# Constants fetched by SyncE in the order of need, the first and last graph's score rows made by TensorE, and the last attention split, in a planned two-layer graph-attention kernel

## The chip, the cores and the metric

The kernel runs as one program on one core of a Trainium2 chip. The core has a tensor engine (PE), a vector engine (DVE), a scalar engine (ACT), a GpSimd engine (POOL) and a sync engine (SP), each with its own stream of instructions, and 16 DMA engines that all queues share. SP, ACT and POOL can issue DMAs. The metric is the device time of one execution in microseconds. Before the change three runs gave 3724.74, 3729.95 and 3728.39 us, with the median 3728.39.

## The reference

There are B = 32 graphs with N = 512 nodes and D = 512 features each, all in float32, and for every graph an integer adjacency of 512 x 512. Two layers follow each other, each in a residual form.

```python
h = relu(layernorm(x))                                    # layer 0
s = (h @ w_src)[:, :, None] + (h @ w_dst)[:, None, :] + attn_b
att = softmax(where(adj + eye == 0, -inf, leaky_relu(s, 0.2)), axis=-1)
x = x + einsum('bij,bjh->bih', att, h)

h = relu(layernorm(x))                                    # layer 1
def gat(x, W, a_src, a_dst, bias):                        # H heads of F features
    xl = (x @ W).reshape(B, N, H, F)
    e = leaky_relu((xl . a_src)[:, :, None, :] + (xl . a_dst)[:, None, :, :], 0.2)
    att = softmax(where((adj > 0) | eye, e, -1e9), axis=1)
    return einsum('bsdh,bshf->bdhf', att, xl) + bias
h = elu(gat(h, W1, ...))                                  # W1 512 x 1024, 4 heads of 256
x = x + gat(h, W2, ...)                                   # W2 1024 x 512, 1 head of 512
```

So each graph has six attentions over 512 x 512 pairs of nodes (one in layer 0, four heads and one more in layer 1), and two products with weights.

## The kernel before

**Per graph.** Nodes lie in T = 4 row blocks of 128 partitions. `layer0_scores` (L695) takes the layernorm statistics of x (L479), writes the normalised and rectified rows h (ACT, L496), makes two score columns for each row block by dot products on DVE (`dot`, L363), loads the adjacency and calls `edge_weights`. `layer0_out` (L714) aggregates and adds to x. `layer1_in` (L719) normalises x again, transposes it on PE into hT, adds b2 to x on POOL and stores x into a DRAM buffer ("spill"). `layer1_project` (L838) multiplies by W1, `layer1_scores` and `layer1_head` (L857, L869) do the attention of a head, its elu and the transposition of its result. `layer2_project` (L912) multiplies by W2, `load_back` (L748) fetches x from DRAM again, and `layer2_out` (L932) does the last attention on it and stores the graph's rows to the output.

**The products with weights** (`products`, L756; the matmul is L808) use seven half-size products in place of eight: four sums of quarters of the left side, made by DVE or POOL (L789, L790), and seven weight factors 11, 21, 22, T1, T2, T3, -T4, of which four are sums made once at the start (`sums`, L449). The products run in that list's order, from 11 to -T4, and results are copied or added out of PSUM (L506, L821). The weights carry two more columns per head, a weight times its attention vector, so that the scores of a node come out of the same product; `scores_1` (32 dots over W1) and `scores_2` (32 over W2, and 8 small sums) make these columns on DVE at the start.

**An attention** (`edge_weights`, L570) needs, for every pair of nodes, the sum of a column value (per partition) and a row value. The two score columns (`ac`) are turned into rows through DRAM: `in_lines` (L535) transposes the columns on PE, copies them to SBUF (`e`) and stores them as lines in DRAM; `row_of` (L552) fetches a line broadcast to all 128 partitions, 256 KB. The row `a_row` is copied by ACT into a PSUM bank (`in_bank`, L564, the copy is L567). DVE adds the mask to it and takes the maximum of each row (L579, four times), then two small steps (L584, L586) give the bound m per node. PE spreads m over the partitions by four transposes of a broadcast column (`spread`, L518; the transpose is L473) into `m_bank`. ACT makes leaky_relu of row plus column from `c_row` (L596), DVE subtracts m (L599), POOL adds the mask, a large negative number where there is no edge (L601), and ACT takes the exponential (L604). `aggregate` (L607, matmul L614) multiplies the weights E by the values; a column of ones beside the values yields the divisor. In `attend` (L621) DVE takes its reciprocal (L626) and adds the quotient to x (L632). Layer 1 does the same for a head with L876 and L879, then ACT's exponential (L888) and DVE's minimum and maximum (L891).

**Masks.** POOL's queue loads an adjacency, converted to bf16 on the way (L650). `masks0` adds the identity to the diagonal blocks (L667) and makes the mask by one DVE operation (L670); `masks1` does it by L682 and L688. SP transposes masks by DMA (`transposed_mask`, L652), four transfers for each.

**What sets the order.** No engine's instructions are written in their final order. Every operation is recorded by `op` with the engines that can do it, a modelled cost (the time its engine is occupied, and the time until its result is there), what it reads and writes, a rank (its position, less `ahead`), and a mark `lock` for operations of DVE and POOL that the model lets exclude each other. `Plan.run` makes six drafts: each is a list scheduling by the modelled costs, in which buffers of a kind are given out as they come free (for most kinds in a fixed turn), and the rank for the next draft is the latest time at which an operation would have to start by the draft before (`latest`). The draft with the shortest modelled end is emitted in its order. Thus a changed cost anywhere can change the order of all engines from beginning to end. In the model each engine is a resource; DMA queues of SP and ACT are two more (SP, ACTQ), and a DMA's bytes occupy nothing: it has only an issue time and a landing time.

**The sequence of recording** is at the end of the kernel (L953 to L988): x of graph 0, the constants, graph 0's layer 0, the weight sums, then a loop over graphs in which the projection of graph b, the last attention of graph b - 1, the four heads of b, layer 0 of b + 1 and b + 2 and the second projection of b are interleaved. A 33rd pass of the loop does only the last attention of graph 31. SBUF has two x buffers, one `h`, one `xl2` and three `pair`; PSUM has six `acc` banks, one `a_bank` and one `m_bank`.

**Constants.** `load_constants` (L371) issues the layer 0 vectors, the attention vectors and the biases from ACT's queue (nine transfers) and the weights from SP (W1 in 8 transfers, W2 in 16).

## Time and profile before

| | |
|---|---|
| runs | 3724.74, 3729.95, 3728.39 us; median 3728.39 |
| the profiled execution | 3721.97 us, of which the span of the profile is 3720.2 us |
| PE (matmul) busy | 3626.9 us, 97% of the span |
| PEld (weight loads) busy | 3134.7 us, 84% |
| DVE busy | 2846.8 us, 77% |
| ACT busy | 1803.5 us, 48% |
| POOL busy | 1627.4 us, 44% |
| DMA | 313.22 MB, mean 84 GB/s |

The span runs from the first to the last profiled event, and the execution's own time is a little longer. PEld overlaps PE. A line such as "15.25 0.29 DVE L667 ... [3.23 <-DMA m<-in_adj_dram]" is an instruction of the timeline: start, duration, engine, source line, operation, output and inputs, and in brackets how long its engine stood idle before it and what ended that. SPq and ACTq rows are the issue of a DMA. A line of waits reads: engine, output and source line that waited, what released it, then the sum in us, the number of such waits and the longest. A line of windows gives a stretch in us and the busy time and count of PE, PEld, DVE, ACT and POOL in it, then the granted clock of the tensor engine as a share of its full speed, the busy share of the DMA engines and the GB/s that they moved.

### The profile page before, as it was taken

The numbers are of one execution on the slowest core, as the hardware profiler recorded it, in microseconds if no ns is written. First come the engines' busy times: TensorE is split into PE (matmuls) and PEld (weight loads), VectorE is DVE, ScalarE is ACT, GpSimd is POOL, SyncE is SP. The second block draws the span as 40 slices with busy tenths as digits, with TensorE's granted clock in tenths as the row PEclk, the third lists the DMA queues.
The fourth block names the chain that finished last, engine by engine and source line by source line (L and its number), as shares of the span: only waits on it lengthen the run. The fifth ranks groups of instructions, "written<-read, shape, count | busy, mean of one in ns | idle before, by whom it ended". The sixth has DMA issues, their size and how long they took to land.

```text
span 3720.2 us, 51279 instructions
## 1 busy us (share of the span) xinstructions
PE 3626.9 (97%) x17792; PEld 3134.7 (84%) x17792; DVE 2846.8 (77%) x7339; ACT 1803.5 (48%) x3339; POOL 1627.4 (44%) x1383
## 2 busy tenths in 40 slices
PE   3899999999999999999999999999999999999998
PEld 2788888888888888888888888888888888888887
DVE  6987778877778777778877787777887777788755
ACT  2454454554445554445544545544455544455433
POOL 3444444444445434444444444444454444444432
PEclk9999999999999999999999999999999999999999
DMA  5244323343323343233443233432233432334311
GB/s 143 65 102 103 72 72 90 75 103 93 71 80 83 85 102 74 77 84 76 101 103 71 73 90 75 103 92 70 80 82 87 103 74 78 83 74 103 91 49 37
DMA packets 305045, 313.22 MB, mean 84 GB/s; under 512 B 150672, under 2 KB 189072, under 8 KB 304784
## 3 DMA queue, kind: packets, MB, share of 16 engines
q1 hardware_dynamic: 269696, 273.49, 27.0%
q0 software_dynamic: 33792, 33.56, 6.9%
q8 instruction: 140, 2.29, 0.3%
q10 hardware_dynamic: 1296, 2.88, 0.2%
q14 instruction: 121, 0.99, 0.1%
HBM read 241.96 MB, written 67.90 MB: 83 GB/s over the span
## 4 chain that ended last, share of the span: by engine, by line
PE 88%; DVE 4%; DMA 3%; ACT 2%; POOL 2%; issue 1%; DVEq 0%; ACTq 0%; POOLq 0%; SPq 0%
PE acc L614 42%; PE acc L808 38%; PE acc L473 5%; PE m_bank L473 2%; DMA m<-in_adj_dram 2%; POOL E_one L601 1%; ACT E L596 1%; DVE junk L364 1%; DMA c_row<-lines 1%; DVE junk L579 1%; DVE E L599 1%; ACT E L604 1%; POOL E L601 0%; PE acc L541 0%; DVE E_one L599 0%
## 5 line engine op out<-in xcount | busy, mean ns | idle before, releaser
L601 POOL TENSOR_TENSOR E<-E,m 128x512 f32<-128x512 f32 x512 | 608.4, 1213 | 856.2 <-DVE E L599 851.6
L614 PE MATMUL acc<-pair,E 128*128 128x257 f32 x4096 | 960.2, 380 | 1.0 <-ACT E L604 0.9
L614 PEld LDWEIGHTS acc<-pair,E 128*128 128x128 f32 x4096 | 751.1, 189 | 104.1 <-ACT E L604 7.7
L808 PE MATMUL acc<-w_T,E 128*128 128x257 f32 (+1 forms) x2048 | 525.7, 380 | 0.0
L614 PE MATMUL acc<-h,E_one 128*128 128x256 f32 (+1 forms) x2048 | 478.9, 381 | 5.2 <-ACT E_one L604 5.2
L614 PE MATMUL acc<-xl,E_one 128*128 128x257 f32 (+1 forms) x2048 | 464.5, 380 | 2.7 <-ACT E_one L604 2.7
L579 DVE CUSTOM_DVE_ANT_0 junk<-m1T,a_bank 128x512 bf16<-128x512 bf16 x640 | 436.5, 682 | 35.1 <-ACT a_bank L567 20.0
L604 ACT ACTIVATE E<-E 128x512 f32<-128x512 f32 x512 | 318.7, 622 | 252.0 <-POOL E L601 250.2
L614 PEld LDWEIGHTS acc<-h,E_one 128*128 128x128 f32 x2048 | 385.7, 191 | 59.7 <-ACT E_one L604 5.9
L614 PEld LDWEIGHTS acc<-xl,E_one 128*128 128x128 f32 x2048 | 384.3, 190 | 59.9 <-ACT E_one L604 3.1
L808 PEld LDWEIGHTS acc<-w_T,E 128*128 128x128 f32 x2048 | 377.0, 190 | 53.2
L596 ACT ACTIVATE E<-c_row,ac 128x512 f32<-128x512 f32 x512 | 343.9, 707 | 3.6 <-DMA c_row<-lines 3.6
L599 DVE TENSOR_TENSOR E<-E,m_bank 128x512 f32<-128x512 f32 x512 | 327.4, 678 | 2.8 <-PE m_bank L473 1.8
L506 ACT COPY xl<-acc 128x257 f32<-128x257 f32 x226 | 84.6, 374 | 502.1 <-PE acc L808 501.8
L506 ACT COPY pair<-acc 128x258 f32<-128x258 f32 x421 | 155.8, 370 | 342.6 <-PE acc L808 342.2
L888 ACT ACTIVATE e<-v,minus_one 128x512 f32<-128x512 f32 x256 | 183.5, 717 | 232.2 <-DVE v L879 172.0
L650 POOL DMA_DIRECT2D m<-in_adj_dram x64 | 51.7, 808 | 546.9 <-DVE col L579 501.4
L632 DVE SCALAR_TENSOR_TENSOR x<-acc,r,x 128x256 f32<-128x256 f32 x512 | 239.5, 479 | 62.1 <-PE acc L614 54.3
L891 DVE SCALAR_TENSOR_TENSOR v<-e,v 128x512 f32<-128x512 f32 x256 | 267.9, 1047 | 13.2 <-ACT e L888 11.4
L808 PE MATMUL acc<-w,hT 128*128 128x258 f32 x1024 | 273.5, 382 | 0.7 <-DVE pair L821 0.6
L808 PE MATMUL acc<-w,pair 128*128 128x257 f32 x1024 | 258.1, 379 | 0.0
L808 PE MATMUL acc<-w,E 128*128 128x257 f32 (+1 forms) x1024 | 254.6, 380 | 0.0
(98 smaller groups left out, 5885.3 us busy)
## 6 DMA issues: line engine op xcount, KB each, us to landing
a_row<-lines SPq DMA_DIRECT2D x192, 256.0 KB, 3.3
c_row<-lines SPq DMA_DIRECT2D x192, 256.0 KB, 3.4
x<-in_x_dram SPq DMA_DIRECT2D x32, 1024.0 KB, 8.5
m<-in_adj_dram POOLq DMA_DIRECT2D x64, 512.0 KB, 7.6
spill<-x SPq DMA_DIRECT2D x32, 1024.0 KB, 4.3
x<-spill SPq DMA_DIRECT2D x32, 1024.0 KB
out_dram<-x SPq DMA_DIRECT2D x32, 1024.0 KB, 5.1
m0T<-m SPq DMA_TRANSPOSE x128, 7.4
```

Source lines behind the costliest of these rows:

```text
L473: op("PE", on_pe(P, transpose=True), lambda: nc.tensor.transpose(dst_of(), src_of(), identity), src, dst(part), ahead)
L506: nc.scalar.copy(dst_of(), src_of())
L579: lambda t=t: nc.vector.tensor_tensor_reduce(junk, mask_max.at[:, t, :], a_row.at, 1.0, LOWEST, ALU.add, ALU.max, accum_out=amax.at[:, t : ...
L596: lambda t=t: nc.scalar.activation(E.at[:, t, :], c_row.at, AF.Prelu, bias=a_of(t), scale=1.0, alpha=SLOPE),
L599: op("DVE", on_dve(N), lambda t=t: nc.vector.tensor_sub(E.at[:, t, :], E.at[:, t, :], m_row.at), m_row(*ROW) + E(t), E(t))
L601: "POOL", on_pool(N, True), lambda t=t: nc.gpsimd.tensor_add(E.at[:, t, :], E.at[:, t, :], mask.at[:, t, :]),
L604: op("ACT", on_act(N), lambda t=t: nc.scalar.activation(E.at[:, t, :], E.at[:, t, :], AF.Exp), E(t), E(t))
L614: lambda s=s: nc.tensor.matmul(acc.at[:, :n], E.at[:, s, node_block(t)], of(s), start=(s == 0), stop=(s == T - 1)),
L632: lambda acc=acc, r=r, f=f, t=t: nc.vector.scalar_tensor_tensor(X.at[:, t, f], acc.at[:, :HD], r.at, X.at[:, t, f], op0=ALU.mult, op1=ALU. ...
L808: lambda k=k: nc.tensor.matmul(acc.at[:, :width], at[a]()[:, k, node_block(r)], weight_of(w, k, c), start=(first and k == 0), stop=(k == n ...
L888: op("ACT", on_act(2 * F, 1), lambda e=e, ts=ts: nc.scalar.activation(e.at, v.at[:, ts, :], AF.Exp, bias=minus_one), parts, e(0))
L891: lambda e=e, ts=ts: nc.vector.scalar_tensor_tensor(v.at[:, ts, :], e.at, 1.0, v.at[:, ts, :], op0=ALU.min, op1=ALU.max),
```

## The change

The planner gets another model of transfers. A DMA that moves data now carries a third cost, its bytes at 300 bytes per ns (`by_dma`), and these occupy one shared resource one after the other (`moving`); of the last `IN_FLIGHT` = 8 transfers the oldest must have landed before another is issued. ACT's own DMA queue is gone from the model.

All constants are fetched by SP. The three small ones of layer 0 are recorded ahead (`AHEAD` = 400), W1 and its attention vectors in their place, and b1, b2, the attention vectors of layer 2 and W2 behind (`LATER` = 300). W2 comes in four transfers in place of 16.

For layer 0 of graph 0 and the last attention of graph 31 the way through DRAM is left out: with `lines` None, `edge_weights` makes both rows by `spread`, four PE transposes each, a into `a_bank` and c into an `acc` bank, and ACT's L596 reads c from PSUM.

The last attention of graph 30 is recorded in two halves: its first two row blocks (`EARLY`) in the loop as before, the other two behind the second projection of graph 31. Then follow the fetch of graph 31's x and its last attention. Graph 31's second projection writes into a `pair` buffer in place of `xl2` (its column of ones is set by a POOL memset), so that graph 30's values can stay. For these last two graphs each row block has an output transfer of its own, 256 KB, in place of one of 1024 KB for a graph.

The operations of the other graphs are the same; their order comes out of the new plan. Lines behind the change have other numbers in the changed kernel: L473 becomes L487, L496 L510, L579 L591, L586 L598, L596 L609, L599 L612, L601 L614, L604 L617, L614 L627, L808 L822, L891 L905.

```diff
-            occupied, there = self.cost(draft, i)
+            occupied, there, *moves = self.cost(draft, i)
             if locks and e in lock:
                 at = max(at, lock["POOL" if e == "DVE" else "DVE"])
                 lock[e] = at + occupied
+            for held in moves:
+                if len(landed) >= self.IN_FLIGHT:
+                    at = max(at, landed[-self.IN_FLIGHT])
+                moving = max(moving, at) + held
+                there += moving - at
+                landed.append(at + there)
...
+def by_dma(n, after=2000.0):
+    return 350.0, after, n / 300.0
...
+    AHEAD, LATER = 400, 300
     QUARTER = (("11", "T1"), ("21", "22"))
     def load_constants():
-        def fetch(queue, ns, place, src, token):
-            engine = {"SP": nc.sync, "ACTQ": nc.scalar}[queue]
-            op(queue, (70.0, ns), lambda: engine.dma_start(place(), src), (), token)
-        fetch("ACTQ", 4000.0, lambda: ws_r, rows(w_src, D), W["w0"](0))
-        fetch("ACTQ", 4000.0, lambda: wd_r, rows(w_dst, D), W["w0"](1))
-        fetch("ACTQ", 4000.0, lambda: b0_r, rows(attn_b, 1), W["w0"](2))
+        def fetch(n, place, src, token, ahead):
+            op("SP", by_dma(4 * P * n), lambda: nc.sync.dma_start(place(), src), (), token, ahead)
+        fetch(D, lambda: ws_r, rows(w_src, D), W["w0"](0), AHEAD)
+        fetch(D, lambda: wd_r, rows(w_dst, D), W["w0"](1), AHEAD)
+        fetch(1, lambda: b0_r, rows(attn_b, 1), W["w0"](2), AHEAD)
         att = [Buffer("E"), Buffer("E")]
         for i, vector in enumerate((att_src1, att_dst1)):
-            fetch("ACTQ", 12000.0, lambda i=i: flat(att[0])[:, i * HF : (i + 1) * HF], rows(vector, HF), att[0](i))
+            fetch(HF, lambda i=i: flat(att[0])[:, i * HF : (i + 1) * HF], rows(vector, HF), att[0](i), 0)
         w1_k = w1.rearrange("(k p) (h f) -> k p h f", p=P, f=F)
         w2_k = w2.rearrange("(k p) f -> k p f", p=P)
         for k in range(KD):
             for half, q in enumerate(QUARTER[k // (KD // 2)]):
                 fetch(
-                    "SP", 10000.0 + 2000.0 * k, lambda k=k, q=q: w1_s[q][:, k % (KD // 2), :, 2:],
-                    w1_k[k, :, half::2, :], W["w1"]((q, k % (KD // 2))),
+                    H // 2 * F, lambda k=k, q=q: w1_s[q][:, k % (KD // 2), :, 2:], w1_k[k, :, half::2, :],
+                    W["w1"]((q, k % (KD // 2))), 0,
                 )
-        fetch("ACTQ", 20000.0, lambda: b1_r, rows(b1, HF), W["b1"](1))
-        fetch("ACTQ", 20000.0, lambda: b2_r, rows(b2, D), W["b2"](0))
+        fetch(HF, lambda: b1_r, rows(b1, HF), W["b1"](1), -LATER)
+        fetch(D, lambda: b2_r, rows(b2, D), W["b2"](0), -LATER)
         for i, vector in enumerate((att_src2, att_dst2)):
-            fetch("ACTQ", 20000.0, lambda i=i: flat(att[1])[:, i * D : (i + 1) * D], rows(vector, D), att[1](i))
-        for k in range(KH):
-            for half, q in enumerate(QUARTER[k // (KH // 2)]):
+            fetch(D, lambda i=i: flat(att[1])[:, i * D : (i + 1) * D], rows(vector, D), att[1](i), -LATER)
+        nk = KH // 2
+        w2_q = w2.rearrange("(i k p) f -> i p k f", p=P, k=nk)
+        for i in range(2):
+            for half, q in enumerate(QUARTER[i]):
                 fetch(
-                    "SP", 16000.0 + 1000.0 * k,
-                    lambda k=k, q=q, half=half: w2_s[q][:, k % (KH // 2), :] if half else w2_s[q][:, k % (KH // 2), 2:],
-                    w2_k[k, :, W2 - 2 :] if half else w2_k[k, :, : W2 - 2], W["w2"]((q, k % (KH // 2))),
+                    nk * HD, lambda q=q, half=half: w2_s[q] if half else w2_s[q][:, :, 2:],
+                    w2_q[i, :, :, W2 - 2 :] if half else w2_q[i, :, :, : W2 - 2], W["w2"](*((q, k) for k in range(nk))), -LATER,
                 )
         op(
...
-        a_row = in_bank("a_bank", row_of("a_row", lines, k))
+        a_row = spread("a_bank", scores, a_of, AHEAD) if lines is None else in_bank("a_bank", row_of("a_row", lines, k))
...
         m_row = spread("m_bank", m(0) + E("place"), lambda t: m.at[:, t : t + 1], AHEAD)
-        c_row = row_of("c_row", lines, k + 1)
+        c_of = lambda t: ac.at[:, k + 1, t : t + 1]
+        c_row = spread("acc", scores + E("place"), c_of, AHEAD) if lines is None else row_of("c_row", lines, k + 1)
...
-                E(s) + values(part(s)) + result("place"), acc(0),
+                E(s) + values(*part(s)) + result("place"), acc(0),
             )
...
-                "SP", (2300.0, 6000.0),
+                "SP", (2200.0, 3000.0, 600.0),
...
-        L0[b] = (h0, edge_weights("E_one", scores, ac, in_lines(ac, scores, 2), 0, m0, m0T))
+        L0[b] = (h0, edge_weights("E_one", scores, ac, in_lines(ac, scores, 2) if b else None, 0, m0, m0T))
...
-        xl = Buffer("xl2")
+        xl = Buffer("xl2" if b < B - 1 else "pair")
+        if b == B - 1:
+            op("POOL", (110.0, 120.0), lambda: nc.gpsimd.memset(xl2_of(xl)[:, :, 2 + D :], 1.0), (), xl(2))
...
-        L2[b] = (edge_weights("E_one", ac(0), ac, in_lines(ac, ac(0), 2), 0, m1T, m1), xl)
-    def layer2_out(b):
-        E, xl = L2.pop(b)
-        Xb = X.pop(b)
-        attend(E, Both(xl), lambda s: s, 2, Xb)
-        op(
-            "SP", (100.0, 5000.0), lambda: nc.sync.dma_start(node_tiles(out, b), Xb.at),
-            Xb(*((t, half) for t in range(T) for half in range(2))), (),
-        )
-    class Both:
-        def __init__(self, buf):
-            self.buf = buf
-        at = property(lambda self: self.buf.at)
-        def __call__(self, s):
-            return self.buf((0, s), (1, s))
+        L2[b] = (edge_weights("E_one", ac(0), ac, in_lines(ac, ac(0), 2) if b < B - 1 else None, 0, m1T, m1), xl)
+    def xl2_of(buf):
+        return buf.at if buf.kind == "xl2" else buf.at[:, : T * (2 + D + 1)].rearrange("p (t f) -> p t f", t=T)
+    def layer2_out(b, ts=ROW, whole=True):
+        E, xl = L2[b]
+        Xb = X[b]
+        attend(E, xl, lambda: xl2_of(xl), lambda s: ((0, s), (1, s), 2), 2, Xb, ts)
+        for block in (ROW,) if whole else [[t] for t in ts]:
+            op(
+                "SP", by_dma(4 * P * len(block) * D),
+                lambda block=block: nc.sync.dma_start(
+                    node_tiles(out, b)[:, block[0] : block[-1] + 1, :], Xb.at[:, block[0] : block[-1] + 1, :]
+                ),
+                Xb(*((t, half) for t in block for half in range(2))), (),
+            )
+    EARLY = T // 2
...
-    for b in range(B + 1):
-        if b < B:
-            masks1(b)
-            layer1_project(b)
+    for b in range(B):
+        masks1(b)
+        layer1_project(b)
         if b:
             load_back(b - 1)
-            layer2_out(b - 1)
-        if b == B:
-            break
+            layer2_out(b - 1, ROW if b < B - 1 else ROW[:EARLY], b < B - 1)
...
+    layer2_out(B - 2, ROW[EARLY:], False)
+    load_back(B - 1)
+    layer2_out(B - 1, ROW, False)
```

## Prediction

> **What bounds the kernel now.** I read the page first, for the bound. Then the waits of PE in three stretches, the windows, and the timelines of start and end.
>
> ```profile
> span 3720.2 us, 51279 instructions
> PE 3626.9 (97%) x17792; PEld 3134.7 (84%) x17792; DVE 2846.8 (77%) x7339; ACT 1803.5 (48%) x3339; POOL 1627.4 (44%) x1383
> ```
>
> The tensor engine is the bound: 97% busy, and the change takes no matrix product away. Only the 3% in which PE has nothing to do can be won. Where do they lie? PE's waits between 190 and 3600 us (first three lines) and before 190 us (the rest):
>
> ```profile
> PE acc L614 <- ACT E L604: 0.9, 5, 0.2
> PE m_bank L473 <- DVE col L586: 0.8, 1, 0.8
> PE acc L541 <- DVE ac L707: 0.2, 1, 0.2
> PE acc L541 <- DVE ac L707: 37.8, 1, 37.8
> PE m_bank L473 <- DVE col L586: 19.8, 2, 18.5
> PE acc L808 <- DVE pair L821: 6.3, 2, 5.6
> PE acc L473 <- ACT h L496: 5.6, 1, 5.6
> PE acc L614 <- ACT E_one L604: 5.2, 2, 2.7
> ```
>
> In 3410 us of middle, PE waits 1.9 us. The idle time is the start and the end. Windows of start and end (busy us of each engine with its count, granted clock, DMA share, GB/s):
>
> ```profile
> 0.00:60.60 60.60, 1.50 (x6) 0.82 (x6) 32.69 (x106) 8.24 (x12) 13.30 (x20) 1.00 0.74 202
> 60.60:186.00 125.40, 109.83 (x495) 92.72 (x496) 111.08 (x312) 56.28 (x103) 62.84 (x48) 0.92 0.24 56
> 3683.40:3697.70 14.30, 5.09 (x24) 3.76 (x22) 6.44 (x16) 4.98 (x10) 1.87 (x2) 0.80 0.11 37
> 3697.70:3720.20 22.50, 16.35 (x64) 13.62 (x64) 4.45 (x12) 1.89 (x3) 2.62 (x3) 0.88 0.13 47
> ```
>
> From 60.6 to 186 us DVE is busy 111.08 of 125.4 us, 89%: there it is nearly as full as PE. The timeline of the start, each line a step of the chain:
>
> ```profile
> 15.25 0.29 DVE L667 TENSOR_TENSOR m<-m,ident 128x128 bf16<-128x128 bf16 x1 [3.23 <-DMA m<-in_adj_dram]
> 21.04 1.28 ACT L496 ACT_TABLE_LOAD   x1 [21.04 <-DMA w<-in_L_gnn_W_dram]
> 30.27 0.69 DVE L479 BATCH_NORM_STATS2 st<-x 128x6 f32<-128x512 f32 x1 [12.95 <-DMA x<-in_x_dram]
> 40.05 0.46 SPq L547 DMA_DIRECT2D lines<-e  x1
> 52.77 0.69 DVE L579 CUSTOM_DVE_ANT_0 junk<-m,a_bank 128x512 bf16<-128x512 bf16 x1 [0.15 <-DVE junk L364]
> 60.58 15.62 PE L614 MATMUL acc<-h,E_one 128*128 128x257 f32 x64 [2.75 <-ACT E_one L604]
> ```
>
> ACT issues loads until 21 us, so its table load and the first normalised rows come late. DVE then stands 12.95 us before the second graph's x. The row's transfer waits until 40.05 us on SP behind three DMA transposes (36.03, 3.92 long). The maximum stands behind weight products on DVE until 52.77. The end:
>
> ```profile
> 3690.50 0.69 DVE L579 CUSTOM_DVE_ANT_0 junk<-m1T,a_bank 128x512 bf16<-128x512 bf16 x1 [2.66 <-ACT a_bank L567]
> 3693.84 1.11 PE L473 MATMUL m_bank<-ident,col 128*128 128x128 f32 x4 [6.46 <-DVE col L586]
> 3697.70 16.35 PE L614 MATMUL acc<-xl,E_one 128*128 128x257 f32 x64 [2.75 <-ACT E_one L604]
> 3714.60 0.39 SPq L938 DMA_DIRECT2D out_dram<-x  x1
> ```
>
> PE is idle 6.46 and 2.75 us, then runs partly at half clock, and 5.6 us follow the last DMA issue.
>
> **Start: the new chain to the first attention.** ACT loses its nine issues; table load and L496 (2.92 us for four) fit before the masks. DVE's order becomes: statistics of graph 0; the first adjacency's diagonal; then the mask of the second adjacency, which is a new wait, with everything of graph 0 queued behind it; the mask of the first; eight score products; two statistics of x of graph 1; the four L579; two more statistics; the maximum. So the unknown is T, the landing of the second adjacency. The first lands at 15.25. Issue to landing is 13.7, 19.8 and 23.9 us for the three first ones; the second is issued at about 2.4 us, so lands near 22.2. T lies between 15.3 and 22.2: fewer bytes go ahead of it now (no attention vectors of layer 2, no b1 and b2, which move behind the weights), but x of graph 1 comes forward to fifth. I take 19.
>
> T 19.0; two masks 2 x 0.69 = 1.4; score products 31.48 to 37.44 = 6.0; bias and handover to PE 0.4; four TensorE transposes at cold clock 1.1 (the 1.11 of m_bank), handover 0.1; four L579, 52.77 to 55.65, 2.9; two statistics 2 x 0.62 = 1.2; two small ones 0.4 (3693.42 to 3693.84); from m_bank to the first product 56.72 to 60.58 = 3.9, and 0.2 for two weight products before the subtraction. Sum 36.6, against 60.58: 24 us earlier (21 to 28 with T). The second four transposes, for c, end 0.9 us later; ACT's four L596 (2.56) end near 31.7, before the subtraction needs them. L596 now reads PSUM: ACT's copies of 128x512 take 0.58 from SBUF (L567) and 0.59 from PSUM (hT), so 0.0 more. The DMA transposes of m0 stand on SP before the last weight piece and wait for the mask at 20.4; four issues of 1.25 and 2.5 to landing make about 28 to 31, needed at 34.7. Behind that wait on SP stand one piece of W1, b1, W2, b2 and the layer 2 vectors, wanted only after 55 us; POOL's next load is not behind it.
>
> **What of the 24 us stays.** DVE had done 32.7 us of work by 60.6. By 36.6 it has done about 20 (the steps above). The 12.7 us left, chiefly 30 of 32 W1 products at 0.47, move under the first attention and into the stretch where DVE was 89% busy. To the state of 186 us DVE's work is 32.7 + 111.1 = 143.8, so 123.8 remain at 36.6. At 89% that takes 139 and 10 us are won; at 100%, 123.8 and 25.6, more than the 24. DVE has 75 of 93 us from 186 on, so some of it can run over into the middle; I take 94%, nearer to the 92.6% (86.10 of 93) of its fullest slice: 132, state reached at 168.3, gain 18 (10 to 24). The two fewer ACT copies and six fewer small DMAs of graph 0 and 31 lie off the path.
>
> **Middle.** Thirty graphs have the same instructions in another order. W2 in four transfers for sixteen frees 12 issues of 0.43 on SP, once. The split last attentions cost no more products. I cost the middle at 0; the cover is that PE's waits there sum to 1.9 us while DVE has 18 us per 93 free.
>
> **End.** Gone: e copy, the line's transfer (1.2), the row's (3.07), a_bank's copy (0.60). Before, from the last -T4 product's end (3683.4) to 3697.7 is 14.3. After: two copies 0.8, ac copy 0.2, handover 0.3, transposes 0.6 warm, L579s 2.9, one added eviction sum 0.43, two small 0.4, then 3.9: 9.6 us, 4.7 less. Against it: after the last -T4, 16 products remained before; now 8, as its place in PE's order is later: 8 x 0.217 = 1.7. Net 3.0 (1 to 4.7). The second half of graph 30's last attention, held back, would be cover for this hole, but in the instruction order it stands before the last heads' attention, and nothing of it in the hole: 0.
>
> Clock: the 64 last products take 16.35 for 64 x 0.217 = 13.9, so 2.4 are lost to half clock, and 0.5 in m_bank. PE's idle pieces become about 3.1 and 3.4 us. Gain 0 to 2.9; 1.2 taken, as 2.75 us of idle shows no switch of its own and 5.6 to 6.5 does.
> The Trainium skill, page "TensorE: Matmul & The Clock Gate", section "Part 1: The HAM clock gate", says a free-running window of about 3.4 us must be idle before the clock is halved. The 6.46 us hole with clock 0.80 agrees; by the rule two pieces of 3.1 and 3.4 would seldom halve it, and the gain would be 2.9.
>
> Output: the last transfer is 256 KB in place of 1024 KB. From issue to end 5.6; a 256 KB row takes 3.07 and 0.5 remains: 2.0 less (0 if only latency counts, 2.5).
> Against splitting speaks the skill, page "DMA: Bandwidth & Descriptors", section "Bandwidth": make transfers of 1 MiB or more. Three of the four go out beside products, so only the last one's length would matter, and by its fit (2.0 us plus bytes over 436 GB/s, an estimate) that is 1.8 less.
>
> **Sum.** 18 + 3.0 + 1.2 + 2.0 = 24.2 us. The profiled execution took 3721.97 (span 3720.2); that gives a span of 3696. It lies 6.4 below the median of the three runs, 3728.39, so in their terms 3704. A measurement tells 0.2% (7.5 us) from no change.
>
> **Rivals.**
> A, slower: the new order brings a wait in every graph. Place: PE's transposes of the maximum (m_bank) behind DVE in the heads, where the order sets a head's L579s between the divisions, activations and minima of the head before. An SBUF operation of DVE stretches beside POOL: L891 is 0.69 alone, 1.05 on average, and one POOL mask addition is 1.21. One such wait unlucky per graph, 1.0 us x 30 = 30: 3704 + 30 = 3734. It turns the sign from 0.8 us per graph. For: the wait already peeps out (0.8 us once), and the old order has been free of it. Against: 18 us of free DVE per 93.
> B, little: DVE stays at 89% through the start, or T is beyond 22: 10 us there and 3 at the end, 3715.
> C: the start gains all 24 and the clock stays up: 24 + 3 + 2.9 + 2 = 32, 3696.
>
> **Chances.** Forecast with C, 3694 to 3714: 0.60. B, 3714 to 3724: 0.20. A, 3721 to 3745: 0.20. Likeliest 3704. The range 3693 to 3731 leaves out half of A, half of a tenth below: under 0.2. Faster: 0.60 + three fifths of B = 0.72, less 0.02 for an unforeseen wait: 0.70; same 0.11; slower 0.19.
>
> **What would show it.** First L614 product (L627 after) at 33 to 40 us; DVE's one wait at the start for an adjacency near 19; no ACT wait for a weight; DVE over 90% busy from 37 to 165; at the end no row transfer, about 10 us from last -T4 to attention, four output transfers of 256 KB. Wrong if PE's waits in the middle exceed 20 us in sum, or the first attention comes after 45.

## The result and the profile after

The changed kernel takes 3693.76 us (median; 3693.08 to 3694.85) against 3726.71 us before (four runs, 3724.74 to 3729.95): a ratio of 0.9911, with the 95% interval 0.9894 to 0.9928. That is 33 us, or 0.9%, faster; the prediction said 3704.0 us, with a range of 3693 to 3731. The profiled execution took 3694.24 us and its span is 3692.5 us, 27.7 us less than the 3720.2 of before. The two differences are not the same number, and that is taken up below.

The page after:

```profile
span 3692.5 us, 51317 instructions
PE 3625.2 (98%) x17806; PEld 3131.3 (85%) x17806; DVE 2878.2 (78%) x7478; ACT 1760.2 (48%) x3227; POOL 1592.1 (43%) x1353
```

PE's busy time is the same within 1.7 us; what went is time in which it had nothing to do. Its waits before 190 us:

```profile
PE a_bank L487 <- DVE junk L378: 26.7, 4, 25.2
PE m_bank L487 <- DVE col L598: 12.9, 4, 5.1
PE acc L487 <- ACT h L510: 7.0, 1, 7.0
PE acc L627 <- ACT E_one L617: 5.3, 2, 2.7
```

The wait for the first score columns begins at zero and ends at 25.2 us, where PE makes the first row itself. Before, PE's first work was at 37.8 us, followed by 18.5 us of waiting for the maximum; now the wait for the maximum is 4.1. The start in lines of the timeline:

```profile
14.08 0.29 DVE L680 TENSOR_TENSOR m<-m,ident 128x128 bf16<-128x128 bf16 x1 [5.24 <-DMA m<-in_adj_dram]
20.80 0.69 DVE L695 TENSOR_SCALAR m<-m 128x2048 bf16<-128x2048 bf16 x1 [4.84 <-DMA m<-in_adj_dram]
22.12 6.62 SPq L669 DMA_TRANSPOSE m0T<-m  x4
29.30 0.67 DVE L591 CUSTOM_DVE_ANT_0 junk<-m,a_bank 128x512 bf16<-128x512 bf16 x1
33.55 1.11 PE L487 MATMUL m_bank<-ident,col 128*128 128x128 f32 x4 [4.12 <-DVE col L598]
37.41 16.46 PE L627 MATMUL acc<-h,E_one 128*128 128x257 f32 x64 [2.74 <-ACT E_one L617]
```

DVE waits three times for a transfer: 4.5 us for graph 0's x, 5.24 for the first adjacency and 4.84 for the second. The last is the new one. SP reaches the mask's transposes at 22.12 in place of 36.03 us, and the first attention begins at 37.41 in place of 60.58, 23.2 us earlier. The end, as windows and as a timeline:

```profile
3663.40:3672.05 8.65, 3.20 (x21) 2.36 (x19) 5.83 (x15) 3.60 (x7) 1.87 (x2) 0.91 0.00 0
3672.05:3692.50 20.45, 16.73 (x64) 13.89 (x64) 4.45 (x12) 1.89 (x3) 2.62 (x3) 0.83 0.14 52
```

```profile
3668.66 0.65 PE L487 MATMUL m_bank<-ident,col 128*128 128x128 f32 x4 [2.71 <-DVE col L598]
3672.05 16.73 PE L627 MATMUL acc<-pair,E_one 128*128 128x257 f32 x64 [2.74 <-ACT E_one L617]
3679.97 9.69 SPq L960 DMA_DIRECT2D out_dram<-x  x4
3688.82 0.48 DVE L645 SCALAR_TENSOR_TENSOR x<-acc,r,x 128x256 f32<-128x256 f32 x1 [1.04 <-PE acc L627]
```

From the last -T4 product to the last attention are now 8.65 us (14.30 before). The wait of 6.46 is 2.71; the 64 products take 16.73 us, 0.38 more than before. From the last DVE operation to the end of the span are 3692.5 - 3689.3 = 3.2 us, where 5.6 followed before.

**Where the 27.7 us went.** To see small stalls too, take all PE instructions of the trace in order and subtract from each distance between two starts the usual one, the median of the middle: 0.2171 us for a pass of a product, 0.109 for a transpose. The rest, summed from the span's start, is called lost time here. The middle has 13,600 passes, so a tenth of a nanosecond in the usual distance shifts its level by 1.4 us in every run alike; only differences between runs are read.

| lost by PE, us | before | after | change |
|---|---|---|---|
| until 200 us | 86.4 | 69.2 | -17.2 |
| 200 to 400 | 2.4 | 4.3 | +1.9 |
| 400 to 3600 | 12.3 | 3.2 | -9.1 |
| 3600 to the end | 19.3 | 14.4 | -4.9 |

The sum is -29.3, and fourteen transposes more cost 14 x 0.109 = 1.5: -27.8. A third of the gain lies in the middle, where the prediction had put nothing. Counted one by one, stalls of more than 0.05 us sum to 10.4 us there before (88 of them, the longest 0.37) and to 1.8 after (29). PE's own waits there were 0.9 us before (1.9 from 190 us on). The waits of the weight loads, in the same stretch of before (400 to 3600 us), show what that view leaves out:

```profile
PEld m_bank L473 <- DVE col L586: 13.3, 57, 0.3
PEld acc L473 <- DVE v L891: 11.1, 27, 0.5
PEld acc L614 <- ACT E L604: 5.0, 15, 0.6
```

and after:

```profile
PEld acc L627 <- ACT E L617: 10.6, 58, 0.2
```

A weight load runs beside the product ahead of it, so a part of its wait costs nothing. But the two kinds of wait for DVE, which come about twice and once in each graph, are gone. One of them in the timeline of before, with the DVE operation that it waited for:

```profile
1044.64 0.69 DVE L891 SCALAR_TENSOR_TENSOR v<-e,v 128x512 f32<-128x512 f32 x1 [0.39 <-ACT e L888]
1045.38 0.14 PEld L473 LDWEIGHTS acc<-ident,v 128*128 128x128 f32 x1 [0.53 <-DVE v L891]
```

The transposes of v stood right behind the DVE operation that makes v. The weight load waited 0.53 us and the stream of PE lost 0.29 of it; a modelled matmul end covers this in PE's own row. Stalls ahead of transposes are 6.5 of the 10.4 us, the rest lies ahead of the heads' products.

### The profile page after: what moved, and what is told of

Its sections match the earlier page's. It is cut to its first block, busy times and chain, and to the rows that moved or that the text cites. A ratio compares the mean times of both kernels' runs of the same rounds, so it can differ in the third digit from the quotient of the medians.

```text
span 3692.5 us, 51317 instructions
## 1 busy us (share of the span) xinstructions
PE 3625.2 (98%) x17806; PEld 3131.3 (85%) x17806; DVE 2878.2 (78%) x7478; ACT 1760.2 (48%) x3227; POOL 1592.1 (43%) x1353
## 4 chain that ended last, share of the span: by engine, by line
PE 94%; DVE 3%; DMA 1%; POOL 0%; issue 0%; ACT 0%; DVEq 0%; ACTq 0%
PE acc L627 46%; PE acc L822 41%; PE acc L487 4%; PE m_bank L487 2%; DVE junk L591 1%; DVE junk L378 0%; PE acc L553 0%; DVE E L612 0%; DMA m<-in_adj_dram 0%; DVE v L905 0%; POOL E_one L614 0%; DVE E_one L612 0%; DMA x<-in_x_dram 0%; DVE v L893 0%; DMA out_dram<-x 0%
## 5 line engine op out<-in xcount | busy, mean ns | idle before, releaser
L614 POOL TENSOR_TENSOR E<-E,m 128x512 f32<-128x512 f32 x512 | 620.2, 1240 | 803.3 <-DVE E L612 798.3
L627 PE MATMUL acc<-pair,E 128*128 128x257 f32 x4096 | 961.6, 381 | 1.4 <-ACT E L617 1.2
L627 PEld LDWEIGHTS acc<-pair,E 128*128 128x128 f32 x4096 | 743.0, 190 | 114.5 <-ACT E L617 14.4
L822 PE MATMUL acc<-w_T,E 128*128 128x257 f32 (+1 forms) x2048 | 521.5, 381 | 1.0 <-ACT pair L522 0.6
L627 PE MATMUL acc<-h,E_one 128*128 128x256 f32 (+1 forms) x2048 | 478.2, 382 | 6.3 <-ACT E_one L617 6.3
L617 ACT ACTIVATE E<-E 128x512 f32<-128x512 f32 x512 | 312.0, 624 | 315.4 <-POOL E L614 315.4
L627 PE MATMUL acc<-xl,E_one 128*128 128x257 f32 x1984 | 448.2, 379 | 0.0
L591 DVE CUSTOM_DVE_ANT_0 junk<-m1T,a_bank 128x512 bf16<-128x512 bf16 x640 | 436.0, 681 | 15.4 <-PE a_bank L487 1.7
L627 PEld LDWEIGHTS acc<-h,E_one 128*128 128x128 f32 x2048 | 383.8, 191 | 59.4 <-ACT E_one L617 7.6
L822 PEld LDWEIGHTS acc<-w_T,E 128*128 128x128 f32 x2048 | 379.6, 190 | 55.4 <-ACT pair L522 0.8
L627 PEld LDWEIGHTS acc<-xl,E_one 128*128 128x128 f32 x1984 | 371.4, 190 | 53.7
L612 DVE TENSOR_TENSOR E<-E,m_bank 128x512 f32<-128x512 f32 x512 | 326.5, 679 | 24.7 <-PE m_bank L487 24.7
L609 ACT ACTIVATE E<-c_row,ac 128x512 f32<-128x512 f32 x512 | 335.6, 708 | 1.9 <-DMA c_row<-lines 1.9
L520 ACT COPY pair<-acc 128x258 f32<-128x258 f32 (+1 forms) x375 | 138.2, 369 | 412.1 <-PE acc L822 410.3
L520 ACT COPY xl<-acc 128x257 f32<-128x257 f32 x219 | 81.7, 373 | 455.8 <-PE acc L822 455.8
L835 DVE TENSOR_TENSOR pair<-acc,pair 128x258 f32<-128x258 f32 (+1 forms) x390 | 164.5, 424 | 137.8 <-PE acc L822 127.7
L822 PE MATMUL acc<-w,hT 128*128 128x258 f32 x1024 | 268.4, 382 | 0.0
L822 PE MATMUL acc<-w,pair 128*128 128x257 f32 x1024 | 259.3, 380 | 0.0
L614 POOL TENSOR_TENSOR E_one<-E_one,m 128x512 f32<-128x512 f32 x128 | 145.0, 1165 | 263.2 <-DVE E_one L612 263.2
```

Of the source, the lines that this page charges most:

```text
L520: nc.scalar.copy(dst_of(), src_of())
L591: lambda t=t: nc.vector.tensor_tensor_reduce(junk, mask_max.at[:, t, :], a_row.at, 1.0, LOWEST, ALU.add, ALU.max, accum_out=amax.at[:, t : ...
L609: lambda t=t: nc.scalar.activation(E.at[:, t, :], c_row.at, AF.Prelu, bias=a_of(t), scale=1.0, alpha=SLOPE),
L612: op("DVE", on_dve(N), lambda t=t: nc.vector.tensor_sub(E.at[:, t, :], E.at[:, t, :], m_row.at), m_row(*ROW) + E(t), E(t))
L614: "POOL", on_pool(N, True), lambda t=t: nc.gpsimd.tensor_add(E.at[:, t, :], E.at[:, t, :], mask.at[:, t, :]),
L617: op("ACT", on_act(N), lambda t=t: nc.scalar.activation(E.at[:, t, :], E.at[:, t, :], AF.Exp), E(t), E(t))
```

## The experiments

"Span" is that of the profiled execution (3692.5 us for the changed kernel, 3720.2 before); lost time as above. The kernel before was run again with each round of experiments, and its medians lie between 3724.6 and 3726.7 us; a difference of less than about 2 us between the medians of two kernels is therefore weak evidence. For the start, four numbers of each run:

| run | first product | DVE idle until 180 us | lost until 400 | span |
|---|---|---|---|---|
| before | 60.6 | 38.9 | 88.8 | 3720.2 |
| flight_16 | 50.0 | 34.8 | 83.0 | 3711.8 |
| uncounted | 42.3 | 30.7 | 81.7 | 3704.9 |
| counted_only | 57.4 | 25.3 | 79.6 | 3703.5 |
| lines_first | 51.6 | 32.6 | 78.4 | 3696.2 |
| act_delay | 41.1 | 27.5 | 74.9 | 3694.1 |
| act_issues | 37.6 | 27.2 | 74.7 | 3694.0 |
| the change | 37.4 | 26.4 | 73.5 | 3692.5 |
| lines_last | 36.4 | 25.9 | 72.4 | 3695.1 |
| unsplit | 36.4 | 26.5 | 72.3 | 3689.9 |
| one_output | 36.3 | 25.7 | 71.7 | 3693.7 |
| late_unsplit | 32.0 | 22.9 | 67.6 | 3685.0 |
| split_forced | 32.1 | 22.4 | 67.1 | 3684.1 |
| mask_late | 31.7 | 23.6 | 66.4 | 3684.6 |

DVE idle is the sum of the gaps between its instructions. Where DVE waits for the second adjacency ahead of the products, that transfer lets it go on between 19.2 and 20.8 us where the constants are SP's (20.8 in the profile of the change), so a first product at 36.4 or 37.4 us is the same thing.

### Constants issued by ACT

```diff
-            op("SP", by_dma(4 * P * n), lambda: nc.sync.dma_start(place(), src), (), token, ahead)
+            op("SP", by_dma(4 * P * n), lambda: queue.dma_start(place(), src), (), token, ahead)
...
+    # queue: nc.scalar for the nine row constants, nc.sync for the weights
```

> The changed kernel with the same plan, but the nine row constants (vectors of layer 0, attention vectors, biases) are issued by ACT at their place in the plan; the weights stay with SP. In the changed kernel ACT's first normalised row starts at 16.0 us and the first score product on DVE at 22.0, because DVE waits for the second adjacency until 20.8. Theory: ACT's issues were not what held the first attention, since DVE stands in that wait anyway; the first product of the first attention (37.4 us in the changed kernel) comes at 37 to 39, and the span (3692.5) grows by 0 to 2 us. Rival: taking the issues off ACT is worth several us; ACT is then busy with issues to about 21 us as in the kernel before, the rows of h end near 24 in place of 19, and the first product comes 4 us later or more, the span 3 us longer or more.

3695.62 us, ratio 0.9920 (0.9907 to 0.9934); span 3694.0. The rows of h begin at 18.4 us in place of 16.0, the first product at 37.6 in place of 37.4, and the span is 1.5 us longer. The theory holds: given this order, who issues the constants is worth 1 to 2 us (1.9 by the medians). DVE's wait covers ACT's delay.

### Graph 0's rows through DRAM

```diff
-        L0[b] = (h0, edge_weights("E_one", scores, ac, in_lines(ac, scores, 2) if b else None, 0, m0, m0T))
+        L0[b] = (h0, edge_weights("E_one", scores, ac, in_lines(ac, scores, 2), 0, m0, m0T))
```

> The changed kernel, planned again, with graph 0's score rows through DRAM as in the kernel before. Theory: the way through DRAM costs more than its own transfers, because the line and the row stand on SP behind four DMA transposes and behind weight pieces; the first product of the first attention comes 12 to 16 us later (49 to 53 us), and about three quarters of it stay in the span: 7 to 12 us more than 3692.5. Rival: it costs the bare chain, a copy 0.4, the line 1.2, the row 3.1, the copy into the bank 0.6, so 5.3 us: first product near 43 and a span 4 us longer.

3697.71 us, ratio 0.9926 (0.9913 to 0.9938); span 3696.2. The first product comes at 51.6 us, 14.2 later, as the theory had it; but only 3.7 us of that are in the span, as the rival had it. Until 200 us 8.7 us more are lost (77.9 against 69.2), until 400 only 4.9. So each expectation misses in one half: the way through DRAM costs far more than its bare transfers at the start, and what follows gives two thirds to three quarters of it back.

### The first attention delayed by itself

```diff
+    def exp(E, t, held):
+        for _ in range(held):
+            nc.scalar.copy(E.at[:, t, :], E.at[:, t, :])
+        nc.scalar.activation(E.at[:, t, :], E.at[:, t, :], AF.Exp)
...
+    # held = 8 for graph 0, layer 0, first row block; 0 elsewhere
```

> The changed kernel with the same plan; before the first exponential of graph 0's first attention ACT copies the same block onto itself eight times (about 0.6 us each, 4.8 in all). DVE and POOL get no more work. Theory: the time of the first attention by itself hardly counts, DVE's idle time does; the first product comes 4.5 to 5 us later (42 us), DVE has other work meanwhile, and the span grows by 0 to 1.7 us. Rival: the first attention is on the path that sets the end, as the prediction had it, with three quarters or more of its shift kept: the span grows by 3.5 to 5 us.

3696.96 us, ratio 0.9924 (0.9911 to 0.9936); span 3694.1. The eight copies:

```profile
35.16 5.17 ACT L586 COPY E_one<-E_one 128x512 f32<-128x512 f32 x8 [4.83 <-POOL E_one L621]
```

The first product comes at 41.1 us. In this execution the second adjacency let DVE go on at 19.23 us, against 19.79 in unsplit and 20.80 in the change. Against unsplit the first product is 4.7 us later and 2.6 us more are lost until 400 (74.9 against 72.3); with the 0.6 us by which the transfer was earlier, 3.2 of 5.3 us. By the medians the run is 3.2 us longer than the change; by span 1.6, which the earlier transfer flatters. So somewhat more than half of the delay stays: more than the theory said, less than the rival. The time of the first attention does count, but not one for one.

### The second adjacency's mask behind the score products

```diff
+        order = list(best.order)
+        for i, j in self.behind:
+            order.remove(i)
+            order.insert(order.index(j) + 1, i)
...
+        if b == 0:   # the mask of masks1(0), behind the bias of graph 0's scores
+            plan.behind.append((len(plan.ops) - 1, SCORED[0]))
```

> The changed kernel with the same plan, but on DVE the mask of the second adjacency, which waits for its transfer until 20.8 us, is emitted behind the eight score products of graph 0 in place of ahead of them. Nothing else moves. Theory: what the start costs is DVE's idle time, since DVE is the fuller engine until about 180 us; DVE's wait of 4.8 us goes, the first product of the first attention comes 4 to 5 us earlier (32.5 to 33.5 us), and 4 to 5 us stay in the span (3687.5 to 3688.5). Rival: the ramp behind it swallows most of it, as it swallowed 10 of the 14 us by which the way through DRAM made the first attention later; then about a third stays, 1 to 2 us.

3688.34 us, ratio 0.9900 (0.9887 to 0.9914); span 3684.6. Two lines of its timeline (the mask is L699 here, the product L631):

```profile
21.82 0.69 DVE L699 TENSOR_SCALAR m<-m 128x2048 bf16<-128x2048 bf16 x1
31.73 8.44 PE L631 MATMUL acc<-h,E_one 128*128 128x257 f32 x27 [2.75 <-ACT E_one L621]
```

The mask no longer has a wait ahead of it. The first product comes 5.7 us earlier than in the change (4.7 earlier than in runs whose second adjacency came a microsecond sooner). The span is 7.9 us shorter, but the profiled execution was the fastest of four; by the medians it is 5.4 us. So nearly all of it stays, unlike in the two runs before. What differs is DVE: here its own idle time falls by 2.8 us until 180, there ACT or the DRAM way held PE while DVE had other work for a part of the time. Where the order of the start is nearly the same (the change, act_issues, act_delay, unsplit, mask_late) the lost time goes with DVE's idle time, but it moves more: 2.8 us less idle go with 7.1 us less lost. Between orders it does not: counted_only has 25.3 us of DVE idle time and loses 79.6. So DVE's idle time is a sign here, and is not shown to be the whole cause.

### The planner without counted transfers

```diff
-    return 350.0, after, n / 300.0
+    return 350.0, after + n / 300.0
```

> The changed kernel, planned again with transfers that occupy nothing in the plan: their bytes only lengthen their landing. All operations stay. The changed kernel loses 4.8 us in PE's stream between 400 and 3600 us over the pure sequence of its products, the kernel before 14.6. Theory: this difference is an accident of which order the plan falls into, not of counting transfers; then the middle loses 2 to 9 us here too, and what changes is the start, with the first product later by 3 to 7 us and the span 0 to 6 us longer. Rival: counting the transfers is what took the small stalls out of the middle; then the middle loses 12 us or more again and the span is 8 us longer or more.

3708.74 us, ratio 0.9955 (0.9942 to 0.9967); span 3704.9: 12.4 us longer, more than the theory allowed and as the rival had it. The middle loses 8.5 us (3.2 in the change). The expectation counted with a slightly smaller usual distance (4.8 for the change, 14.6 before); with 0.2170 us for a pass this run loses 10.1 where the change loses 4.9 and the kernel before 13.9, above the theory's 9 and below the rival's 12. The start loses 8.2 us more until 400, and its timeline tells why:

```profile
26.35 1.34 SPq L391 DMA_DIRECT2D w<-in_L_gnn_W_dram  x1
31.07 6.92 SPq L669 DMA_TRANSPOSE m0T<-m  x4
40.33 5.16 POOL L614 TENSOR_TENSOR E_one<-E_one,m0T 128x512 f32<-128x512 f32 x4 [0.74 <-DVE junk L378]
42.31 16.02 PE L627 MATMUL acc<-h,E_one 128*128 128x257 f32 x64 [13.16 <-ACT E_one L617]
```

Where transfers occupy nothing, the plan issues all of W2 first, since that is free in the model, and graph 0's mask transposes stand behind it on SP until 31.07 us (22.12 in the change). PE then waits 13.16 us for the masked weights. (The masks' transposes, which have a cost of their own, still count in this plan.) In the middle the plan is another order on every engine but SP.

### Sixteen transfers in flight

```diff
-    IN_FLIGHT = 8
+    IN_FLIGHT = 16
```

> The changed kernel, planned again with at most 16 transfers in flight in the plan in place of 8; the bytes still occupy one resource. Theory: of the model's two parts the limit sets the start, because it makes SP's places dear: with 16 the plan issues all weight pieces of both layers ahead of the four transposes of graph 0's first mask, POOL's mask additions wait for these, and the first product comes at 45 to 50 us in place of 37.4; the span is 4 to 9 us longer. In the middle another order comes out, with 3 to 9 us lost. Rival: the counted bytes set the order at the start, and the limit does nothing: the first product at 36 to 39 us, the span within 2 us of 3692.5.

3712.91 us, ratio 0.9965 (0.9952 to 0.9977); span 3711.8: 19.3 us longer. In its timeline:

```profile
30.66 6.33 SPq L669 DMA_TRANSPOSE m0T<-m  x4
47.96 5.22 POOL L614 TENSOR_TENSOR E_one<-E_one,m0T 128x512 f32<-128x512 f32 x4
50.01 10.26 PE L627 MATMUL acc<-h,E_one 128*128 128x257 f32 x36 [16.24 <-ACT E_one L617]
```

The first product is at 50.0 us and the start loses 9.5 us more until 400, as expected; here, too, W2 is issued ahead of the mask's transposes. The span's forecast, 4 to 9 us, misses, because the middle loses 13.3 us, more than the kernel before and out of the expected range. Yet it is no other order: from 400 to 3400 us the instructions of every engine follow each other as in the trace of the change, by line, tile and shape. What differs is one start of DVE in each graph, here (the first two lines) and in the change (the last two):

```profile
458.27 0.60 PE L487 MATMUL m_bank<-ident,col 128*128 128x128 f32 x4
459.34 2.48 DVE L612 TENSOR_TENSOR E<-E,m_bank 128x512 f32<-128x512 f32 x4 [0.92 <-PE m_bank L487]
```

```profile
448.73 0.60 PE L487 MATMUL m_bank<-ident,col 128*128 128x128 f32 x4
449.43 2.48 DVE L612 TENSOR_TENSOR E<-E,m_bank 128x512 f32<-128x512 f32 x4 [0.55 <-PE m_bank L487]
```

DVE goes on 0.47 us behind the end of PE's transposes here, 0.10 in the change, and PE then stalls for the head's weights. It is the same instruction in 27 graphs, every 256th of DVE's stream, late by 0.35 us on average, and 27 x 0.35 = 9.5 of the 10.1 us. In the 14 profiles of this case, with 104,560 DVE instructions, 39 start more than 0.2 us (0.32 to 0.47) behind both the event that they waited for and the instruction ahead. Counted along DVE's stream, all 39 stand at the same place in 128. What happens there is not shown. The plan's other start shifted DVE's stream so that this place fell on an instruction for which the heads wait. So the limit of 8 set the order of the start; for the order of the middle 16 did as well.

### The counted transfers alone, on the kernel before

```diff
+    IN_FLIGHT = 8
...
+            for held in moves:
+                if len(landed) >= self.IN_FLIGHT:
+                    at = max(at, landed[-self.IN_FLIGHT])
+                moving = max(moving, at) + held
+                there += moving - at
+                landed.append(at + there)
...
+def by_dma(n, after=2000.0):
+    return 350.0, after, n / 300.0
...
-            "SP", (350.0, 5500.0),
+            "SP", by_dma(4 * P * N, 4500.0),
+    # and so for the other transfers and the masks' transposes; constants stay with ACT and SP, W2 in 16 pieces
```

> The kernel before with the new planner's model of transfers alone: bytes counted in one resource, at most 8 in flight, the new costs of the transfers and of the transposed masks; the constants stay with ACT and SP in their pieces, all rows through DRAM, no split. Theory: the model of transfers orders the start better by itself, first product at 52 to 57 us in place of 60.6, and 6 to 10 us less are lost by 200 us; the middle is whichever order comes out, 3 to 13 us lost; the end as before. The span is 3701 to 3715. Rival: without the constants on SP the model brings nothing at the start, first product within 2 us of 60.6, and the span stays within 3 us of 3720.

3705.80 us, ratio 0.9946 (0.9932 to 0.9959); span 3703.5, 16.7 us less than before. Until 400 us 9.2 us less are lost, in the middle 8.8 less (3.5 against 12.3), at the end 1.2 more. The theory holds but for the first product, 57.4 us where 57 was the bound, and the size is the news: the planner's model of transfers (bytes, limit and new costs together) brings 16.7 of the 27.7 us, and all of the middle's gain. The plans with bytes and a limit of 8 (the change, lines_first, unsplit, lines_last, late_unsplit, counted_only) lose 3.2 to 3.8 us in the middle (split_forced, planned the same way, has the waits that it moves into the last heads just ahead of 3600 us). But these are not six cases: from 400 to 3400 us DVE, ACT, POOL and SP have one and the same order in all of them, and in flight_16, and only PE's differs a little in lines_first and counted_only. Two other orders, those of the kernel before and of uncounted, lose 12.3 and 8.5. That this order has fewer stalls is shown; that counted bytes lead to such an order in general, and not by chance in this plan, is not.

### Graph 31's rows through DRAM

```diff
-        L2[b] = (edge_weights("E_one", ac(0), ac, in_lines(ac, ac(0), 2) if b < B - 1 else None, 0, m1T, m1), xl)
+        L2[b] = (edge_weights("E_one", ac(0), ac, in_lines(ac, ac(0), 2), 0, m1T, m1), xl)
```

> The changed kernel, planned again with the score rows of graph 31's last attention through DRAM as in the kernel before. Theory (the prediction's term): copy, line, row and copy into the bank stand on the path, 4.0 to 5.0 us; PE's wait for the maximum, 2.7 us in the changed kernel, becomes 6.5 to 7.5, and the span grows to 3696.5 to 3697.5. Rival: the products still to be made cover the transfers: the span grows by under 1.5 us.

3696.82 us, ratio 0.9920 (0.9906 to 0.9934); span 3695.1. PE's wait for the maximum:

```profile
3670.61 1.11 PE L487 MATMUL m_bank<-ident,col 128*128 128x128 f32 x4 [6.46 <-DVE col L598]
```

It is the 6.46 us of before again, and from 3600 us to the end 18.7 us are lost in place of 14.4: 4.3 us, as expected. The span grew by 2.6 only and misses its forecast (3696.5 at least), because the start of this execution was a microsecond better; by the medians it is 3.1.

### One output transfer for a graph

```diff
-        lambda block=block: nc.sync.dma_start(
-            node_tiles(out, b)[:, block[0] : block[-1] + 1, :], Xb.at[:, block[0] : block[-1] + 1, :]
-        ),
+        lambda block=block: nc.sync.dma_start(node_tiles(out, b), Xb.at) if block[-1] == T - 1 else None,
```

> The changed kernel with the same plan; the last two graphs' rows go out in one transfer of 1024 KB each, issued where the last of the four stood. Theory: the time after the last DVE operation is set by the length of the last transfer; it was 3.2 us after that operation in the changed kernel, and is 2.0 us longer here (5.1 to 5.6 us from issue to end), so the span is 3694.5. Rival: latency alone counts and the four pieces gain nothing: the span is within 0.5 us of 3692.5.

3695.34 us, ratio 0.9919 (0.9905 to 0.9932); span 3693.7. The last DVE operation ends at 3688.40 us, so 5.3 us follow it, 2.1 more than in the change, as expected. The span is only 1.2 us longer, because this start lost 1.8 us less. The length of the last transfer sets the time after the last DVE operation.

### The last attention of graph 30 not split, and its half forced into the hole

```diff
-        layer2_out(b - 1, ROW if b < B - 1 else ROW[:EARLY], b < B - 1)
+        layer2_out(b - 1, ROW, b < B - 1)
...
-    layer2_out(B - 2, ROW[EARLY:], False)
```

> The changed kernel, planned again without the split of graph 30's last attention; the four output transfers for graph 31 stay. Theory: the held-back half fills nothing of the two holes before the last attention (2.7 and 2.7 us), and PE's idle time at the end stays; the span is within 1.5 us of 3692.5. Rival: the half, 16 products of 0.43 us, was cover for the end; without it the span is 3 us longer or more.

3691.54 us, ratio 0.9908 (0.9895 to 0.9922); span 3689.9. The two holes at the end stay as they are, 2.7 us each, and from 3600 us on 12.5 us are lost in place of 14.4. The split does not cover the holes; it costs about 2 us (2.2 by the medians), of which a wait of PE for v (L905), 1.3 us, is gone here. The span, 2.6 us shorter, misses the theory's bound of 1.5; 1.2 us of it lie in the start.

```diff
+                E(s) + values(*part(s)) + result("place") + list(after), acc(0),
...
-    layer2_out(B - 2, ROW[EARLY:], False)
+    layer2_out(B - 2, ROW[EARLY:], False, L2[B - 1][1]((0, 0)))
```

> The changed kernel with the late mask of the second adjacency (3684.6 us by itself), planned again with one more dependency: the held-back half of graph 30's last attention may start only after the first result of graph 31's second projection, so that it can lie in the hole before the last attention. Theory: there is no spare work at the end; the two holes of 2.7 us go, but the heads of graph 31, from which the half is taken, get as much idle time, 4 to 6 us in sum: the span stays within 2 us of 3684.6. Rival: the half was only placed badly; in the hole it saves 3 to 5 us: 3680 to 3681.5.

3687.18 us, ratio 0.9896 (0.9882 to 0.9909); span 3684.1, against 3684.6 without the dependency. PE's waits from 3560 us on:

```profile
PE acc L633 <- ACT E L623: 4.7, 3, 2.3
PE acc L633 <- ACT E_one L623: 1.4, 1, 1.4
PE acc L493 <- DVE v L921: 0.4, 1, 0.4
```

The wait for the maximum is gone and the one for the last weights halved, but the heads now wait 4.7 us for their weights, as the theory had it. The half attention is cover wherever it stands, and there is only one of it.

### The mask late and no split

```diff
+            plan.behind.append((SECOND, DOTS, 7))
...
-        layer2_out(b - 1, ROW if b < B - 1 else ROW[:EARLY], b < B - 1)
+        layer2_out(b - 1, ROW, b < B - 1)
```

> The changed kernel with two edits: the mask of the second adjacency behind graph 0's score products on DVE, and no split of graph 30's last attention. Theory: the two act in different stages and add up: the first product at 31 to 33 us, PE's idle time at the end as in the run without the split, the span 3681 to 3683. Rival: what the start gains is taken back by the end or the middle: the span is no shorter than the 3684.6 of the first edit alone.

3685.43 us (3685.05 to 3686.78), ratio 0.9891 (0.9878 to 0.9905); span 3685.0. By span it is no shorter than mask_late's 3684.6, so the rival's bound is met and the expected 3681 to 3683 is missed; by the medians it is 2.9 us shorter. The profiled execution of mask_late was its fastest, the one here its slowest. Its median is the lowest of all, 8.3 us below the change's, where the two edits by themselves have 5.4 and 2.2; so the medians speak for adding up and the spans do not show it.

## Why the prediction was right, and where it was not

The direction and the range held, the range by under 1 us at its lower end; the measured 3693.76 lies just below the 3694 to 3714 to which the prediction gave 0.60. That the sum of 24.2 came within 3.5 us of the measured 27.7 is partly luck: the start gave 2.7 less than forecast, the end 1.3 less and added transposes took 1.5, while the middle, put at nothing, gave 9.1. Of the rivals, C's number, 3696, came nearest, but not by its way: the start did not keep all 24 us and the clock did not stay up. DVE did not stay at 89%, as B had it.

**The start** was right step by step. T, taken as 19 between 15.3 and 22.2, was 20.80; the chain's sum, 36.6, was 37.41, since the chain behind T took 16.6 us in place of 17.6. DVE's wait for the second adjacency came ahead of all of graph 0 as forecast. DVE was to be 94% busy afterwards, and from 37.4 to 180 us it is busy 133.64 of 142.6 us, 93.7%. Of the 23.2 us, 17.2 remained at 200 us (18 forecast), and 15.3 at 400. But the prediction let the first attention's time carry this. The experiments put a weaker tie there: a delay of it cost a good half (act_delay) or about a quarter (lines_first), while nearly all of a shift stayed that came with less idle time of DVE (mask_late). It also gave the start to the constants on SP and the rows from PE. Those count, 1.5 and 3.7 us of span when undone; but uncounted, which keeps both, loses 8.2 us of the start again, and counted_only has 9.2 of the 15.3 us without either. The order that comes from the new model of transfers was the larger part, and the prediction named it nowhere as a cause.

**The middle is the step that failed.** "I cost the middle at 0; the cover is that PE's waits there sum to 1.9 us": these waits did not show stalls of 0.05 to 0.37 us that came in nearly every graph. Lost time there was 12.3 us before and 3.2 after, a gain of 9.1. Rival A, a new wait of 1 us in each graph, did not happen in the change. In flight_16 one of 0.35 us came in each graph, at m_bank too, but with the same order as in the change: by the place of an instruction in DVE's stream. That this place meets no instruction for which the change waits is luck; nothing in its plan looks after it.

**The end** was forecast at 3.0 + 1.2 + 2.0 = 6.2 us and gave 4.9. PE's idle part of the hole went from 14.30 - 5.09 = 9.21 to 8.65 - 3.20 = 5.45 us: 3.8 (3.0 forecast, and 4.3 by lines_last). The output gave 2.5 (2.0 forecast; 2.1 by one_output). The prediction's other estimate, 1.8, takes its fit from the Trainium skill, page "DMA: Bandwidth & Descriptors", section "Anatomy of one DMA — SWDGE (gpsimd) path", which gives it for DMAs issued by GpSimd; SP issues these, and the measured 2.1 decides. The clock gave nothing: the 64 products took 16.73 us in place of 16.35. The trace has the granted clock at half from 3670.55 to 3677.38 us, after two holes of 2.71 and 2.74 us with 0.65 us of transposes between them. The Trainium skill, page "TensorE: Matmul & The Clock Gate", section "Part 1: The HAM clock gate", would have the clock halved after an idle window of about 3.4 us, and neither hole is that long; the measurement decides. A single hole of 2.71 us can be enough: in one_output the clock is at half from 3666.61 us, 2.4 us into the first hole, and the transposes behind it take 1.11 us in place of 0.65:

```profile
3666.91 1.11 PE L487 MATMUL m_bank<-ident,col 128*128 128x128 f32 x4 [2.71 <-DVE col L598]
```

With the same two holes the 64 products took 15.5 (mask_late, uncounted) to 17.1 us (one_output, act_delay). In split_forced a single hole of 1.45 us left the clock up, and the 64 products took 14.12. The split, costed at 0, cost about 2.

**The level.** The prediction added 6.4 us to its span, by which the profiled execution of before lay below the median. After, the profiled execution is 0.5 us above the median. Of the 10.2 us between 3704.0 and 3693.76, about 3.5 are the gain that was sized too small and about 7 are this. The kernel before spreads over 8 us (3721.8 to 3729.95 in all runs), and the change over 1.8; its profiled execution (3721.97) was one of its fastest. Whether the small stalls of its middle make that spread was not tried.

## What to carry to other kernels

Where PE is 97% busy, also read the waits of the weight loads, and the distance between the same instruction in two repetitions: a stall of 0.3 us in each of 30 repetitions hides behind a modelled matmul end and is worth a third of this change. Before a difference is put down to another order, compare the orders: in flight_16 they were the same. In a planner a transfer that costs nothing is issued as early as it can be, ahead of one that is wanted sooner; here its bytes and a limit of 8 on those in flight were both needed to put the mask's transposes ahead of W2. A filler taken to one hole opens another, so ask where it came from; and an earlier start is not worth what the first product moves, but a quarter of it to nearly all, so look at what the fullest engines stand idle.

## What was not expected of the hardware

Two idle stretches of 2.7 us with 0.65 us of work between them were enough for 6.83 us at half clock, in the change as in unsplit and late_unsplit (half clock 6.83 us in each); in one_output the first alone was enough, and half clock lasted 10.24 us; one of 1.45 us was not. All 39 late starts of DVE (0.32 to 0.47 us behind the end of their wait) stood at one place in 128 instructions of its stream; since a graph has 256 DVE instructions in this order, such a place can meet the same instruction in every graph. And the second adjacency, loaded by the same instruction in the change's own plan, let DVE go on at 19.23 us (act_delay), 19.63 (one_output) and 20.80 (the change), one profiled execution each; the first product of one_output comes 1.16 us earlier with it.
